# Blocks of two chunks in the attention layer of a four-layer graph kernel

## The chip, the cores and the metric

The kernel runs on one core of a Trainium2 chip, as one program and one launch. The metric is the device time of an execution in microseconds (us). The engines of a core run their own queues and meet at semaphores: TensorE (matmuls into PSUM), VectorE (elementwise work), ScalarE (copies and activations), GpSimd, and SyncE, which issues most transfers. In the profile they are PE, DVE, ACT, POOL and SP; PEld is TensorE's load of weights, the stationary operand.

## The reference, cut to what matters

Four layers update `x` (2708 rows of 256). Each adds a graph operation to `x` and normalises the rows. The change lies in layer 1, attention of four heads of 64 over the edges of `adj`:

```python
h = (x @ W).reshape(n, heads, head_dim)
src = jnp.einsum('nhd,d->nh', h, a[:head_dim, 0])
dst = jnp.einsum('nhd,d->nh', h, a[head_dim:, 0])
e = src[:, :, None] + dst.T[None, :, :]
e = jnp.where(e > 0, e, ALPHA * e)
e = jnp.where(adj[:, None, :] > 0, e, NEG_INF)
attn = jax.nn.softmax(e, axis=-1)
out = jnp.einsum('nhm,mhd->nhd', attn, h).reshape(n, heads * head_dim)
out = (out - mu) / jnp.sqrt(var + LN_EPS) * gamma + beta
```

For every row and head a sum of weighted rows of `h` is needed, and the total of the weights, its denominator.

## The kernel before

The 2708 rows are 22 tiles of 128 (the last has 20 rows). The program is traced with a framework that assigns buffers, sets semaphores and orders each engine's queue by a planner: an instruction earlier in the program goes first, but one whose operands are ready in the plan can be put ahead of it. A pool with `bufs=n` for a tag hands out n buffers in turn; a tile that takes a used buffer waits for its last reader.

**What layer 1 holds.** The exponential of the leaky logit splits into a factor of the row and a factor of the column, and a maximum of two such products. `rise` has a column value per neighbour and head (a chunk is one tile of 128 neighbours, on the partitions); `fall_b` has the row factors of a group of rows, the same on all partitions, loaded from the DRAM tensor `fall_d` by `load_fall` (L418 to L421); `mask` says where an edge is. One VectorE instruction (L835) makes the weights of a chunk of neighbours for all rows of a group and one head, the tile `p`: the larger of `fall_b` and `rise`, times `mask`. `hs[c]` holds, for each head, the rows of `h` of chunk c, scaled, with the scale itself as an added column.

**Groups and passes.** The rows are taken in groups of two spans, `for g in range(0, len(spans), 2)` (L786): spans of 512 and 512 rows, again 512 and 512, and last 384 and 276. A group makes two passes over the 22 chunks, one for each pair of heads q (L810), so there are six passes. In a pass each chunk does:

- two weight tiles `p` (heads 2q and 2q+1) on VectorE, from a pool of five buffers (L834);
- `heads` (L814): for both spans and both heads a matmul with 64 columns of `hs` as the weights and a span's columns of `p` as the moving operand, into accumulators `acc[s]`. The two heads fill two halves of the array side by side;
- `totals` (L822): the same with the last 32 columns of a head's `hs`, whose last column gives the denominator. The four of a chunk (two spans, two heads) fill four quarters side by side and go into one accumulator `den`.

Each such matmul is two instructions on TensorE[...]. The order of the parts turns at each chunk (L841): totals then heads for even chunks, heads then totals for odd ones, so that equal parts of neighbouring chunks meet.

After the first part of a chunk, `step(c)` (L796) does one piece of other work: in the first group what remains of layer 0, in later ones the end of the group before (`layer1_end`, L683, and `layer1_logits`, L748: transposes and small matmuls on TensorE, a few instructions on VectorE, many on ScalarE). For the first pair of heads it starts a piece where c leaves 1 when divided by 5, for the second where c is a multiple of 5.

**End of a pass.** ScalarE copies `acc` to `sum` (L848) and `den` to `den0` and `den1` (L852). The pool of accumulators has four banks, a pass uses three, and the next pass takes what is free.

**Row factors.** `falls` (L623) holds two tiles of four heads by 1024 columns, loaded on GpSimd's queue as soon as layer 0 has done their rows (L449). The third group's takes the first one's buffer, on SyncE's queue (L789 to L792).

After the last pass the memory of layer 1 goes to `raw_sums` (L354), whose loads `pa` start layer 2.

Of the kernel before, what the change touches and what calls it, by code (L numbers as in the profile page):

```python
# [9 lines left out]
F32 = mybir.dt.float32  # L10
# [5 lines left out]
ALU = mybir.AluOpType  # L16
# [3 lines left out]
P = 128  # L20
# [7 lines left out]
def kernel(  # L28
# [24 lines left out]
    nc = tc.nc  # L53
    N, F = x.shape
    NT = -(-N // P)
    FC = F // P
    HD = a1.shape[0] // 2
    H = F // HD
# [3 lines left out]
    W = GT * P  # L62
    CT = 32
# [6 lines left out]
    spans = [(sum(sizes[:i]), sum(sizes[: i + 1])) for i in range(len(sizes))]  # L70
# [21 lines left out]
    def width(lo, hi):  # L92
        return min(hi * P, N) - lo * P
# [9 lines left out]
                yield t, a, b  # L103
            lo -= sz(t)

    def bcast_rows(d, lo, n):

        return bass.AP(tensor=d.tensor, offset=d.offset + lo, ap=[[0, P], [d.shape[1], d.shape[0]], [1, n]])

    def pool(name, bufs=1, **kw):  # L110
        return tc.tile_pool(name=name, bufs=bufs, reuse_waits="tile", **kw)
# [32 lines left out]
    fall_d = dram.tile([H, N], F32, name="fall_d")  # L144
# [253 lines left out]
    mask = mask_pool.tile([P, NT, MP], FP8, name="mask")  # L398
# [5 lines left out]
    if True:  # L404
# [6 lines left out]
        rise = keep.tile([P, NT, H], F32, name="rise")  # L411
# [3 lines left out]
        ps_t = ps_t_stack.enter_context(pool("ps_t", 4, space=PSUM, side="right"))  # L415
        ps_acc = acc_stack.enter_context(pool("ps_acc", 4, space=PSUM))
        if True:
            def load_fall(dst, g, queue):  # L418
                at, w = spans[g][0] * P, width(*spans[g])
                off = at - spans[g - g % 2][0] * P  # L420
                queue.dma_start(dst[:, :, off : off + w], bcast_rows(fall_d, at, w))  # L421

            def layer1_projection(pool, t):
                n = sz(t)
                xt = transposed(ps_t, pool, xs[t], n, "xt")
                yield
                pm = ps_t.tile([P, 4, P], F32, tag="tr", name="pm").rearrange("p i q -> p (i q)")
                for f in range(FC):
                    nc.tensor.matmul(
                        pm[:n, : F + 2 * H], xt[:, f, :n], w1_a[:, f], start=(f == 0), stop=(f == FC - 1)  # L430
                    )
                nc.scalar.activation(rise[:n, t, :], pm[:n, F + H : F + 2 * H], AF.Exp, scale=1.0 - ALPHA)
                nc.scalar.activation(hs[t][:n, :, HD], pm[:n, F + H : F + 2 * H], AF.Exp, scale=ALPHA)
                fall = pool.tile([P, H], F32, tag="fall", name="fall", bufs=4)
                nc.scalar.activation(fall[:n], pm[:n, :H], AF.Exp, scale=ALPHA - 1.0)
                nc.vector.tensor_tensor(
                    hs[t][:n, :, :HD],
                    pm[:n, H : H + F].rearrange("p (h d) -> p h d", d=HD),
                    hs[t][:n, :, HD:].to_broadcast([n, H, HD]),
                    ALU.mult,  # L440
                )
                yield
                pf = ps_t.tile([P, 4, P], F32, tag="tr", name="pf")
                nc.tensor.transpose(pf[:H, 0, :n], fall[:n], ident[:n, :n])
                turned = pool.tile([H, P], F32, tag="turned", name="turned")
                nc.scalar.copy(turned[:, :n], pf[:H, 0, :n])
                nc.gpsimd.dma_start(fall_d[:, t * P : t * P + n], turned[:, :n])

                for g in [g for g, (lo, hi) in enumerate(spans[:4]) if hi == t + 1]:  # L449
                    load_fall(falls[g // 2], g, nc.gpsimd)  # L450

            w0_b = keep.tile([P, F], F32, name="w0_b")
            quarter = keep.tile([P, CT], F32, name="quarter")
# [2 lines left out]
            with pool("l0", 2) as l0:  # L456
# [48 lines left out]
                with pool("prep", side="right") as prep:  # L505
# [3 lines left out]
                    for c0, c1 in blocks:  # L509
                        whole = min(c1, N // P)  # L510
                        queue = nc.scalar if c1 <= 3 else nc.sync
# [33 lines left out]
                    for f in range(FC):  # L545
                        for s in range(2):
# [7 lines left out]
                            at = s * (H + F)  # L554
# [50 lines left out]
                    t = ahead + 1  # L605
# [14 lines left out]
                gamma_b = keepr.tile([P, F], F32, name="gamma_b")  # L620
                beta_b = keepr.tile([P, F], F32, name="beta_b")
                fallp = fall_stack.enter_context(pool("fallp", 2, side="right"))
                falls = [fallp.tile([P, H, 2 * W], F32, tag="fall_b", name="fall_b") for _ in range(2)]  # L623
                nc.sync.dma_start(gamma_b, bcast(gamma, F))
                nc.sync.dma_start(beta_b, bcast(beta, F))
                layer0_scale(ahead, last)
# [10 lines left out]
                t = NT - 1  # L637
# [23 lines left out]
            if True:  # L661
# [124 lines left out]
                for g in range(0, len(spans), 2):  # L786
                    segs = spans[g : g + 2]
                    at, w = segs[0][0] * P, width(segs[0][0], segs[-1][1])
                    if g >= 4:  # L789
                        falls.append(fallp.tile([P, H, 2 * W], F32, tag="fall_b", name="fall_b"))  # L790
                        for i in range(len(segs)):
                            load_fall(falls[-1], g + i, nc.sync)  # L792
                    cols = [(lo * P - at, width(lo, hi)) for lo, hi in segs]
                    sums, steps, halves = [], [itertools.chain(*rest)] if g == 0 else [], []

                    def step(c):  # L796
                        for s in list(steps):
                            if next(s, s) is s:
                                steps.remove(s)

                        if q == 0 and c % 5 == 1 and len(halves) < len(ended):
                            halves.append(layer1_end(l1, ended[len(halves)]))
                            next(halves[-1])
                            steps.append(itertools.islice(halves[-1], 2))

                        if q == 1 and c % 5 == 0 and c // 5 < len(halves):
                            steps.append(itertools.chain(halves[c // 5], [None], layer1_logits(ended[c // 5])))
                            next(steps[-1])

                    for q in range(H // 2):  # L810
                        den = ps_acc.tile([P, W], F32, tag="acc", name="den")
                        acc = [ps_acc.tile([P, W], F32, tag="acc", name="acc") for _ in segs]

                        def heads(c, ps, flags):  # L814
                            for s, (p0, ws) in enumerate(cols):
                                for i in (1, 0):
                                    nc.tensor.matmul(  # L817
                                        acc[s][i * HD : (i + 1) * HD, :ws], hs[c][:, 2 * q + i, :HD],
                                        ps[i][:, p0 : p0 + ws], **flags,
                                    )  # L820

                        def totals(c, ps, flags):  # L822
                            for s, (p0, ws) in enumerate(cols):
                                for i in (1, 0):
                                    j = (2 * (s ^ q) + i) * CT
                                    nc.tensor.matmul(  # L826
                                        den[j : j + CT, :ws], hs[c][:, 2 * q + i, HD + 1 - CT :],
                                        ps[i][:, p0 : p0 + ws], **flags,
                                    )

                        for c in range(NT):
                            ps = []
                            for i in range(2):
                                p = l1.tile([P, 2 * W], F32, tag="p", name="p", bufs=5)  # L834
                                nc.vector.scalar_tensor_tensor(  # L835
                                    p[:, :w], falls[g // 2][:, 2 * q + i, :w], rise[:, c, 2 * q + i : 2 * q + i + 1],
                                    mask[:, c, at : at + w], ALU.max, ALU.mult,
                                )
                                ps.append(p)

                            for part in (heads, totals)[:: -1 if c % 2 == 0 else 1]:  # L841
                                part(c, ps, dict(start=(c == 0), stop=(c == NT - 1)))
                                if part is (totals, heads)[c % 2]:
                                    step(c)
                        got = []
                        for s, (p0, ws) in enumerate(cols):
                            sb = keepr.tile([P, W], F32, tag=f"sum{q}{s}", name=f"sum{q}{s}")
                            nc.scalar.copy(sb[:, :ws], acc[s][:, :ws])  # L848
                            got.append(sb)
                        for s, (p0, ws) in enumerate(cols):  # L850
                            two = slice(2 * (s ^ q) * CT, 2 * ((s ^ q) + 1) * CT)
                            nc.scalar.copy(dens[s][two, :ws], den[two, :ws])  # L852
                        sums.append(got)
                    for a in steps:
                        for _ in a:
                            pass
                    ended = [(t, s, sums, dens, t - segs[0][0]) for s, (lo, hi) in enumerate(segs) for t in range(lo, hi)]
                    ended = [ended[i : i + 2] for i in range(0, len(ended), 2)]
# [842 lines left out]
```

## Time and profile before

| | |
|---|---|
| median of three runs | 1865.03 us (1864.9 to 1866.25) |
| profiled execution, its own time | 1865.35 us |
| its span (first to last instruction) | 1863.6 us |
| granted TensorE clock | 0.998 |
| layer 1, first totals to last | 247.06 to 590.5 us, 343.4 us |

The six passes, each from its first totals matmul to that of the next (busy us):

| pass | from to | length | PE | DVE | ACT |
|---|---|---|---|---|---|
| group 1, heads 0 and 1 | 247.06 to 308.31 | 61.25 | 61.25 | 56.87 | 1.98 |
| group 1, heads 2 and 3 | 308.31 to 368.31 | 60.00 | 60.00 | 54.75 | 2.41 |
| group 2, heads 0 and 1 | 368.31 to 431.36 | 63.05 | 63.05 | 60.58 | 26.15 |
| group 2, heads 2 and 3 | 431.36 to 497.46 | 66.10 | 66.10 | 54.01 | 9.31 |
| group 3, heads 0 and 1 | 497.46 to 542.33 | 44.87 | 44.87 | 42.86 | 22.57 |
| group 3, heads 2 and 3 | 542.33 to 590.50 | 48.17 | 47.94 | 37.99 | 11.53 |

In a row of the profile's tables of groups stand line, engine, operation, output and inputs, tile shape and count, then busy time in us, mean ns of one, and the idle time before it with what ended it. In the order of time a row begins with start and duration in us. A PE matmul that is called 128*64 uses 128 partitions and 64 columns of weights. Matmuls overlap, so their durations can't be added; starts can be compared.

### The profile page before, as it was taken

Reading aid. Unit: us, or ns where it says so; the run is one execution under the profiler, and the core shown is the slowest. Engines: PE = TensorE matmul, PEld = TensorE weight load, DVE = VectorE, ACT = ScalarE, POOL = GpSimd, SP = SyncE. Lnnn points to the kernel's source line nnn. Section 1 sums busy time; section 2 is a strip of 40 time slices with the busy share of each in tenths; the row PEclk is TensorE's granted clock in tenths of the full one; section 3 lists DMA queues with packets and bytes.
Section 4 is the critical chain, followed back from the end, with each engine's and each line's share of the span. In section 5 each row is a group of like instructions: output and inputs, shape, how many; then the busy total and the mean of one; then the engine's idle time right before and its main releaser. Section 6 shows DMA issues by size and latency. Waiting matters only on the chain. (4 is left out here: it accounts for less than half of the span.)

```text
span 1863.6 us, 23088 instructions
## 1 busy us (share of the span) xinstructions
PE 1832.7 (98%) x7526; PEld 1035.4 (56%) x7530; DVE 1280.9 (69%) x2263; ACT 699.3 (38%) x1442; POOL 266.4 (14%) x427
## 2 busy tenths in 40 slices
PE   9999999999999999999999999999999999999997
PEld 7788832233345887887444444444445556654555
DVE  5344489999897664754568888776887768844664
ACT  3544410033144203111546655555665556321011
POOL 1211220001012411000002000111200302111111
PEclk9999999999999999999999999999999999999999
DMA  8344410100002667754647666454554545634764
GB/s 298 133 148 151 168 30 1 30 1 12 12 7 71 144 144 186 182 130 114 182 131 207 176 174 171 123 159 114 165 151 121 135 106 141 167 106 116 203 163 121
DMA packets 435101, 237.32 MB, mean 127 GB/s; under 512 B 184363, under 2 KB 422348, under 8 KB 432540
## 3 DMA queue, kind: packets, MB, share of 16 engines
q1 hardware_dynamic: 422414, 208.66, 41.4%
q0 software_dynamic: 8208, 22.59, 3.9%
q10 hardware_dynamic: 4350, 4.50, 0.7%
q8 instruction: 62, 1.02, 0.2%
q14 instruction: 67, 0.55, 0.1%
HBM read 223.00 MB, written 12.66 MB: 126 GB/s over the span
## 5 line engine op out<-in xcount | busy, mean ns | idle before, releaser
L835 DVE SCALAR_TENSOR_TENSOR p<-fall_b,rise,mask 128x1024 f32<-128x1024 f32 (+1 forms) x264 | 293.9, 1156 | 32.5 <-PE den L826 16.7
L1328 ACT ACTIVATE p<-st,e_neg 128x1024 f32<-128x1024 f32 (+1 forms) x198 | 197.3, 1040 | 193.9 <-PE m L328 190.1
L328 PE MATMUL m<-s,xq 128*128 128x512 f32 (+3 forms) x660 | 230.1, 467 | 0.0
L817 PE MATMUL acc<-p,h 128*64 128x512 f32 (+2 forms) x1056 | 214.5, 548 | 0.2 <-ACT sum L848 0.2
L328 PE MATMUL m<-p,xq 128*128 128x512 f32 (+1 forms) x396 | 183.0, 544 | 0.1
L215 PE MATMUL acc<-turn,strip 128*128 128x257 f32 x792 | 181.8, 379 | 0.0
L1331 ACT ACTIVATE p<-p 128x1024 f32<-128x1024 f32 (+1 forms) x198 | 178.8, 942 | 0.2
L315 DVE TENSOR_TENSOR s<-p 128x512 f32<-128x512 f32 (+3 forms) x132 | 81.5, 618 | 136.6 <-PE m L328 112.7
L328 PE MATMUL m<-p,x 128*128 128x512 f32 (+1 forms) x396 | 167.7, 542 | 0.3 <-DVE supt L345 0.3
L328 PEld LDWEIGHTS m<-s,xq 128*128 128x128 f32 x660 | 124.5, 190 | 76.3 <-issue 59.2
L1332 DVE TENSOR_TENSOR p<-p,blk 128x1024 f32<-128x1024 f32 (+1 forms) x132 | 142.8, 1101 | 33.6 <-ACT p L1331 23.1
L215 PEld LDWEIGHTS acc<-turn,strip 128*128 128x128 f32 x792 | 147.2, 190 | 20.3
L817 PEld LDWEIGHTS acc<-p,h 128*64 128x64 f32 x1056 | 69.8, 136 | 138.2 <-issue 128.6
L328 PE MATMUL m<-s,x 128*128 128x512 f32 (+3 forms) x330 | 127.2, 467 | 0.0
L826 PE MATMUL den<-p,h 128*32 128x512 f32 (+2 forms) x1056 | 117.8, 548 | 0.0
L328 PEld LDWEIGHTS m<-p,xq 128*128 128x128 f32 x396 | 74.6, 190 | 76.9 <-issue 61.3
L328 PEld LDWEIGHTS m<-p,x 128*128 128x128 f32 x396 | 74.8, 190 | 75.5 <-issue 61.1
L474 ACT ACTIVATE below<-strip 128x384 bf16<-128x384 f32 x132 | 78.4, 594 | 68.4 <-DMA strip<-in_adj_t_dram 65.0
L316 DVE TENSOR_TENSOR p<-p 128x512 f32<-128x512 f32 (+3 forms) x132 | 82.3, 624 | 2.3
L328 PEld LDWEIGHTS m<-s,x 128*128 128x128 f32 x330 | 62.0, 190 | 39.2 <-issue 34.6
L318 DVE TENSOR_TENSOR s<-p,s 128x512 f32<-128x512 f32 (+3 forms) x132 | 81.2, 615 | 1.9
L286 POOL TENSOR_TENSOR blk<-blk,offdiag 128x128 f32<-128x128 f32 (+3 forms) x50 | 28.2, 566 | 376.0 <-DMA blk<-in_adj_t_dram 359.2
(288 smaller groups left out, 2591.9 us busy)
## 6 DMA issues: line engine op xcount, KB each, us to landing
strip<-in_adj_t_dram SPq DMA_DIRECT2D x19, 1408.0 KB, 6.0
blk<-in_adj_t_dram SPq DMA_DIRECT2D x88, 256.0 KB, 3.4
blk<-in_adj_t_dram SPq DMA_DIRECT2D x88, 192.0 KB, 4.1
pa<-in_adj_t_dram SPq DMA_DIRECT2D x110, 128.0 KB, 2.8
turn<-in_adj_t_dram SPq DMA_DIRECT2D x44, 256.0 KB, 3.1
blk<-in_adj_t_dram SPq DMA_DIRECT2D x88, 128.0 KB, 2.7
p<-in_adj_t_dram SPq DMA_DIRECT2D x88, 128.0 KB, 2.7
turn<-in_adj_t_dram SPq DMA_DIRECT2D x44, 192.0 KB, 3.1
```

The lines of the kernel that those rows point to most:

```text
L215: at = nc.tensor.matmul(acc, s[:, c, :n], rhs(c), start=(c == 0), stop=(c == NT - 1))
L315: nc.vector.tensor_tensor(s1, a21, a22, ALU.add)
L316: nc.vector.tensor_tensor(a21, a21, a11, ALU.subtract)
L318: nc.vector.tensor_tensor(s4, a12, s2, ALU.subtract)
L328: nc.tensor.matmul(dst[:, :w], lt, rt, start=start and not (one_bank and i), stop=stop and not (one_bank and i in (1, 2, 5)))
L474: nc.scalar.activation(below[:, : (hi - lo) * P], s[:, lo:hi].rearrange("p c n -> p (c n)"), AF.Relu, scale=-1.0, accum_out=negative[:, BE ...
L817: nc.tensor.matmul(acc[s][i * HD : (i + 1) * HD, :ws], hs[c][:, 2 * q + i, :HD], ps[i][:, p0 : p0 + ws], **flags,)
L826: nc.tensor.matmul(den[j : j + CT, :ws], hs[c][:, 2 * q + i, HD + 1 - CT :], ps[i][:, p0 : p0 + ws], **flags,)
L835: nc.vector.scalar_tensor_tensor(p[:, :w], falls[g // 2][:, 2 * q + i, :w], rise[:, c, 2 * q + i : 2 * q + i + 1], mask[:, c, at : at + w] ...
L1328: nc.scalar.activation(p[:, :, :w], st_k[:, :, :w], AF.Relu, scale=-1.0, bias=e_neg[:, at, k : k + 1])
L1331: nc.scalar.activation(p[:, :, :w], p[:, :, :w], AF.Exp, scale=-1.0)
L1332: nc.vector.tensor_tensor(p[:, :, :w], p[:, :, :w], blk[:, i, :, :w], ALU.mult)
```

## The change

Layer 1's chunks are taken in blocks of two. An even block does the totals of both chunks, then the heads of both; an odd block heads, then totals. `step` is called after the first part for the first chunk and after the second part for the second. The pool of `p` has nine buffers in place of five. A tile of `fall_b` holds only the two heads of one pass; the two of the first group are loaded in layer 0, and each later one at the end of the pass that used its buffer. In the last group the totals no longer follow the spans of 384 and 276 rows but stretches of 320 and 340, and the copies of `den` put the rows back to their spans; in the other groups the stretches are 512 and 512, as before.

```diff
-    def bcast_rows(d, lo, n):
+    def bcast_rows(d, row, rows, lo, n):
 
-        return bass.AP(tensor=d.tensor, offset=d.offset + lo, ap=[[0, P], [d.shape[1], d.shape[0]], [1, n]])
+        return bass.AP(tensor=d.tensor, offset=d.offset + row * d.shape[1] + lo, ap=[[0, P], [d.shape[1], rows], [1, n]])
...
-            def load_fall(dst, g, queue):
+            def load_fall(dst, g, q, queue):
...
-                queue.dma_start(dst[:, :, off : off + w], bcast_rows(fall_d, at, w))
+                queue.dma_start(dst[:, :, off : off + w], bcast_rows(fall_d, 2 * q, 2, at, w))
...
-                for g in [g for g, (lo, hi) in enumerate(spans[:4]) if hi == t + 1]:
-                    load_fall(falls[g // 2], g, nc.gpsimd)
+                for g in [g for g, (lo, hi) in enumerate(spans[:2]) if hi == t + 1]:
+                    for q, dst in enumerate(falls):
+                        load_fall(dst, g, q, nc.gpsimd)
...
-                falls = [fallp.tile([P, H, 2 * W], F32, tag="fall_b", name="fall_b") for _ in range(2)]
+                falls = [fallp.tile([P, 2, 2 * W], F32, tag="fall_b", name="fall_b") for _ in range(H // 2)]
...
-                    if g >= 4:
-                        falls.append(fallp.tile([P, H, 2 * W], F32, tag="fall_b", name="fall_b"))
-                        for i in range(len(segs)):
-                            load_fall(falls[-1], g + i, nc.sync)
                     cols = [(lo * P - at, width(lo, hi)) for lo, hi in segs]
+                    cut = min(cols[1][0], (w // 2 + P // 4) // (P // 2) * (P // 2))
+                    halves_at = [(0, cut), (cut, w - cut)]
...
                         def totals(c, ps, flags):
-                            for s, (p0, ws) in enumerate(cols):
+                            for s, (p0, ws) in enumerate(halves_at):
...
-                        for c in range(NT):
-                            ps = []
-                            for i in range(2):
-                                p = l1.tile([P, 2 * W], F32, tag="p", name="p", bufs=5)
-                                nc.vector.scalar_tensor_tensor(
-                                    p[:, :w], falls[g // 2][:, 2 * q + i, :w], rise[:, c, 2 * q + i : 2 * q + i + 1],
-                                    mask[:, c, at : at + w], ALU.max, ALU.mult,
-                                )
-                                ps.append(p)
-
-                            for part in (heads, totals)[:: -1 if c % 2 == 0 else 1]:
-                                part(c, ps, dict(start=(c == 0), stop=(c == NT - 1)))
-                                if part is (totals, heads)[c % 2]:
-                                    step(c)
+                        fall_b = falls.pop(0)
+                        for b, c0 in enumerate(range(0, NT, 2)):
+                            block = {}
+                            for c in range(c0, min(c0 + 2, NT)):
+                                block[c] = []
+                                for i in range(2):
+                                    p = l1.tile([P, 2 * W], F32, tag="p", name="p", bufs=9)
+                                    nc.vector.scalar_tensor_tensor(
+                                        p[:, :w], fall_b[:, i, :w], rise[:, c, 2 * q + i : 2 * q + i + 1],
+                                        mask[:, c, at : at + w], ALU.max, ALU.mult,
+                                    )
+                                    block[c].append(p)
+
+                            for i, part in enumerate((heads, totals)[:: -1 if b % 2 == 0 else 1]):
+                                for c, ps in block.items():
+                                    part(c, ps, dict(start=(c == 0), stop=(c == NT - 1)))
+                                if c0 + i < NT:
+                                    step(c0 + i)
+                        if g + 2 < len(spans):
+                            falls.append(fallp.tile([P, 2, 2 * W], F32, tag="fall_b", name="fall_b"))
+                            for i in range(len(spans[g + 2 : g + 4])):
+                                load_fall(falls[-1], g + 2 + i, q, nc.sync)
...
-                            nc.scalar.copy(dens[s][two, :ws], den[two, :ws])
+                            for i, (a, n) in enumerate(halves_at):
+                                lo, hi = max(p0, a), min(p0 + ws, a + n)
+                                if lo < hi:
+                                    part = slice(2 * (i ^ q) * CT, 2 * ((i ^ q) + 1) * CT)
+                                    nc.scalar.copy(dens[s][two, lo - p0 : hi - p0], den[part, lo - a : hi - a])
```

## The prediction

> **What bounds the kernel now.** I read the page first, then the table of the span by stretches, then the order of time on TensorE and on its weight loads inside layer 1, and last the waits. The page's busy line and its two largest groups of layer 1:
>
> ```profile
> PE 1832.7 (98%) x7526; PEld 1035.4 (56%) x7530; DVE 1280.9 (69%) x2263; ACT 699.3 (38%) x1442; POOL 266.4 (14%) x427
> ...
> L835 DVE SCALAR_TENSOR_TENSOR p<-fall_b,rise,mask 128x1024 f32<-128x1024 f32 (+1 forms) x264 | 293.9, 1156 | 32.5 <-PE den L826 16.7
> ...
> L817 PE MATMUL acc<-p,h 128*64 128x512 f32 (+2 forms) x1056 | 214.5, 548 | 0.2 <-ACT sum L848 0.2
> ```
>
> TensorE (PE) is busy all the time and waits for nobody; VectorE (DVE) waits 32.5 us, for TensorE to give weight tiles back. A busy TensorE still says nothing of gaps inside it, so I go to the order of time. TensorE in the pass of the second group, first pair of heads:
>
> ```profile
> 380.99 3.65 PE L817 MATMUL acc<-p,h 128*64 128x512 f32 x16
> 384.57 1.92 PE L826 MATMUL den<-p,h 128*32 128x512 f32 x16
> ...
> 387.23 3.65 PE L817 MATMUL acc<-p,h 128*64 128x512 f32 x16
> 390.82 1.93 PE L826 MATMUL den<-p,h 128*32 128x512 f32 x16
> 392.67 3.65 PE L817 MATMUL acc<-p,h 128*64 128x512 f32 x16
> ```
>
> Every program matmul is two instructions, so x16 is two chunks. The reader is to see strict alternation: heads of two chunks, totals of two chunks. Now the weight loads of one such pair of runs:
>
> ```profile
> 380.99 0.20 PEld L817 LDWEIGHTS acc<-p,h 128*64 128x64 f32 x4 [0.84 <-issue]
> 381.47 0.14 PEld L817 LDWEIGHTS acc<-p,h 128*64 128x64 f32 x2 [0.29 <-issue]
> 381.90 0.14 PEld L817 LDWEIGHTS acc<-p,h 128*64 128x64 f32 x2 [0.29 <-issue]
> ...
> 384.57 0.16 PEld L826 LDWEIGHTS den<-p,h 128*32 128x32 f32 x8 [0.81 <-issue]
> 385.03 0.13 PEld L826 LDWEIGHTS den<-p,h 128*32 128x32 f32 x4 [0.30 <-issue]
> ...
> 386.43 0.20 PEld L694 LDWEIGHTS tr<-ident,sum 128*128 128x128 f32 x2 [0.84 <-issue]
> ```
>
> Loads inside a run start 0.43 us apart: one slot of 512 columns, two heads matmuls or four totals matmuls side by side. A run of heads over two chunks is 8 slots, 3.44 us, but lasts 380.99 to 384.57, 3.58; a run of totals is 4 slots, 1.72, but lasts 1.86, to the first transpose of other work at 386.43. Each change of kind thus costs 0.14 us beyond its slots. In the last group the slot of 384 columns is 0.32 us; runs there start thus:
>
> ```profile
> 537.90 1.49 PE L826 MATMUL den<-p,h 128*32 128x384 f32 x16
> 539.32 2.44 PE L817 MATMUL acc<-p,h 128*64 128x384 f32 x16
> ```
>
> Totals: 1.42 us for 4 slots of 0.32 and one change. The 276-column matmuls of the totals set nothing; they run beside the 384-column ones.
>
> Check by sum: a wide pass is 22 x (4 + 2) x 0.43 + 22 x 0.14 = 59.8 us, and the second pass, which has no other work in it, is 60.0 long. So layer 1 is slots plus changes, with no stall.
>
> **What the Trainium skill says.** "TensorEngine Tiling (Array Packing)", section Tiling Modes, Key Properties: "Changing tiling mode (not just tile) drains the TensorE". It gives no price; this trace agrees and prices it at 0.14 us. "TensorE: Matmul & The Clock Gate", Part 3, says that column tiles run concurrently while matmuls start and end in program order; the trace agrees: four 32-column totals share one slot. "Trainium Kernel Development and Optimization", Performance Expectations, warns that matmul busy time measures little since matmuls are pipelined; hence the weight loads above. No page that I use bears on the weight-tile buffers.
>
> **The change, part by part.**
>
> *Blocks of two chunks.* Even blocks do totals of two chunks, then heads of two; odd blocks the reverse. Equal kinds of neighbouring blocks join, so a run is four chunks long. Eleven blocks have eleven inner changes, and one more falls between passes (a pass now ends with heads and starts with totals): 12 against 22. Six passes x 10 x 0.14 us = 8.4 us off TensorE.
>
> *Stretches of 320 and 340.* A totals slot in the last group falls from 384 to 340 columns. At 0.43/512 = 0.84 ns a column, 44 columns x 2 slots = 0.074 us a chunk, x 44 chunks of two passes = 3.25 us off.
>
> *Steps inside a run.* The planned extra work (transposes, small matmuls of L694, L756, L773) is called after the first and the second part of a block. Before, every such place was a change of kind anyway. Now the second is inside a run of four chunks, and the work breaks it: one more change. In the passes that carry the end of the former group the calls that use TensorE come at chunks 1, 6, 11, 16 (first pair) and 4, 5, 9, 10, 14, 15, 19, 20 (second pair); half are odd chunks, 12 in all over two groups, and some 2 for the last rows of layer 0 in the first pass: 14 x 0.14 = 2.0 us back.
>
> *End of a pass.* Before, the last run was totals of one chunk, so the ScalarE copies of the sums went beside it. Now heads end last; the four copies (0.59 us each, 2.4 with a wake of 0.25 makes 2.6) must free accumulators while the next pass does two chunks of totals, 1.72 + 0.28 us. If the heads wait for two sums alone, that is hidden; if for all four copies, 0.6 us late. Nothing to 3.1 us over five ends; I take 0.2 each, 1.0. The third denominator copy in the last group sits on ScalarE, busy 34.1 us of the 93.0 in those passes: nothing.
>
> *Nine weight buffers.* A block holds four tiles until its second part, so five would not carry it; nine hold the block and 2.5 chunks ahead. VectorE's need is what could take over. By pass of the last two groups:
>
> ```profile
> 368.31:431.36 63.05, 63.05 (x380) 18.80 (x376) 60.58 (x86) 26.15 (x128) 8.44 (x7) 1.00 0.04 13
> 431.36:497.46 66.10, 66.10 (x404) 21.81 (x400) 54.01 (x48) 9.31 (x25) 6.34 (x9) 1.00 0.06 17
> 497.46:542.33 44.87, 44.87 (x382) 20.36 (x378) 42.86 (x80) 22.57 (x119) 5.16 (x5) 1.00 0.00 1
> 542.33:590.50 48.17, 47.94 (x404) 23.21 (x394) 37.99 (x55) 11.53 (x34) 10.05 (x20) 1.00 0.07 22
> ```
>
> Length, then busy PE, weight loads, DVE, ACT and POOL. The third pass needs 60.6 us of VectorE and will have 63.05 - 1.4 + 0.3 = 61.95 of TensorE: still TensorE, by little. The fifth needs 42.9 and will have 44.87 - 1.4 - 1.63 + 0.3 = 42.1: VectorE falls 0.8 us behind, from a lead of 2.5 chunks, where a chunk of 660 columns is 1.72 us of VectorE. The lead mostly covers it: 0.5 us, between nothing and 3.0 if an epilogue instruction blocks weights behind it. Gain from the deeper buffers: TensorE's few waits for p are 4.5 us in sum at most 0.3 long, mostly inside a slot; I count none, at best 1.5.
>
> *Row factors.* Six half-sized tiles in place of three: the same bytes. Two heads are loaded on SyncE's queue at the end of each of the first four passes, after VectorE's last read of the slot, and needed one whole pass (about 60 us) later; such a load lands in 5.5 to 6.6 us, and that queue stands idle in layer 1. On GpSimd's queue in layer 0 it is still four loads, of half the size. Nothing. It would cost up to 6 us a pass only were the load placed behind something on SyncE that waits for the end of layer 1; none is there before 590.77.
>
> Sum: 8.4 + 3.25 - 2.0 - 1.0 - 0.5 = 8.15 us. The stages after layer 1 start when its last matmul frees buffers (their first loads go out at 590.77, 0.3 us after it) and TensorE is the bound there too, so all shifts with it. Against the profiled execution, 1865.35 (1863.6 of span and 1.75 around it): 1857.2. The median of the runs is 0.3 lower, 1865.03: 1856.9.
>
> **Rivals.**
>
> *VectorE and the accumulators take part of it back.* Both upper bounds come in: 3.1 for 1.0 and 3.0 for 0.5. Gain 3.55 us, 1861.5. For: the narrow margins of the third and fifth pass. Against: the second pass of each group leaves VectorE idle 10 us or more, which refills its lead.
>
> *The drain is not saved.* If the 0.14 us comes back inside longer runs (weights queued too late), only 3.25 - 1.5 is left: 1863.3. Against: inside the present runs the step over a chunk's end shows no gap, 0.43 throughout.
>
> *The order is not the written one (slower).* The planner that orders the queues is free to take heads of a chunk that are ready before totals of the next that are not. If each chunk's totals and heads then alternate, TensorE changes 44 times a pass: 22 x 6 x 0.14 = 18.5 us more, less 3.25: 1880. It decides from about 24 changes a pass on, where 12 extra changes eat the remaining 1.75 us. For: it does reorder; VectorE works on L727 at 379.99, a whole pass ahead of its place in the program. Against: that hoisting shows weights planned well ahead of TensorE, and TensorE itself runs in written order in every pass before.
>
> **How the numbers follow.** Forecast 0.66, first rival 0.12, second 0.10, third 0.10, better than all bounds 0.02. The forecast's own ends are 1853.9 (no cost at the ends of passes or from VectorE, 1.5 gained by buffers) and about 1860. The range 1853.5 to 1863.5 takes in the first two rivals and leaves out the third: some 0.86. A measurement of this kernel tells 0.2%, 3.7 us, from no change: below 1861.3 lie the forecast, half of the first rival and the rest, 0.74; within are the other half and the second rival, 0.16; slower is the third, 0.10.
>
> **What would show it.** Right: TensorE runs of x32 for heads and totals in the middle of a pass, 0.43 apart inside; the second pass 58.5 long; totals of the last group 0.57 a chunk; layer 1 ending near 582. Wrong: waits of TensorE for p or for the sums' copies above 3 us in sum, VectorE without idle time in the third or fifth pass, runs of x8, or a later start of the first matmul on pa than 3.3 us after layer 1.

## The result, and the profile after

| | before | after |
|---|---|---|
| median of 18 runs each, side by side | 1866.07 us (1863.38 to 1869.16) | 1859.25 us (1856.86 to 1865.58) |
| ratio, with its 95% interval | | 0.9968 [0.9961, 0.9975] |
| profiled execution, its own time | 1865.35 us | 1862.97 us |
| its span | 1863.6 us | 1861.2 us |

The changed kernel is faster by 0.32%, some 6.0 us, where 8.15 us were forecast. The means of the 18 runs differ by 6.05 us, the medians by 6.82. The forecast of 1856.9 us lies 2.35 us below the median.

The page of after, in the lines that answer to those of before (busy lines, then groups: busy time, mean ns of one, idle time before and its cause):

```profile
PE 1825.8 (98%) x7530; PEld 1040.5 (56%) x7530; DVE 1275.9 (69%) x2263; ACT 699.3 (38%) x1444; POOL 266.6 (14%) x427
...
L837 DVE SCALAR_TENSOR_TENSOR p<-fall_b,rise,mask 128x1024 f32<-128x1024 f32 (+1 forms) x264 | 288.0, 1153 | 25.7 <-PE den L825 15.1
...
L816 PE MATMUL acc<-p,h 128*64 128x512 f32 (+2 forms) x1056 | 210.1, 547 | 0.0
```

The picture is the old one: TensorE has no idle time of its own before the heads, and VectorE still waits for weight tiles to come back, now 25.7 us instead of 32.5. So VectorE has not become the bound. This page can't show more, since the saved drains were counted as busy.

The table of after by stretches, one row for each pass (length, busy PE, weight loads, DVE, ACT, POOL, granted clock, DMA share, GB/s):

```profile
250.45:312.42 61.97, 61.97 (x363) 17.59 (x362) 59.31 (x59) 2.63 (x9) 4.98 (x6) 1.00 0.09 26
312.42:370.80 58.38, 58.38 (x355) 17.21 (x353) 53.14 (x46) 2.33 (x4) 0.00 (x0) 1.00 0.06 19
370.80:432.69 61.89, 61.89 (x379) 19.55 (x377) 59.68 (x83) 25.76 (x126) 8.20 (x6) 1.00 0.04 12
432.69:497.78 65.09, 65.09 (x403) 22.48 (x401) 54.03 (x54) 9.78 (x26) 7.22 (x10) 1.00 0.09 28
497.78:540.01 42.23, 42.23 (x377) 21.11 (x376) 38.64 (x70) 20.00 (x110) 4.71 (x4) 1.00 0.00 1
540.01:588.62 48.61, 47.06 (x402) 24.09 (x401) 35.94 (x59) 14.53 (x45) 11.02 (x20) 0.96 0.07 20
```

Against the passes of before, and against what the prediction's terms give for each (0.14 us for ten changes, the cut, the broken runs, 0.2 for an end, 0.5 for VectorE in the fifth):

| pass | before | after | change | forecast |
|---|---|---|---|---|
| 1 | 61.25 | 61.97 | +0.72 | -0.92 |
| 2 | 60.00 | 58.38 | -1.62 | -1.20 |
| 3 | 63.05 | 61.89 | -1.16 | -0.92 |
| 4 | 66.10 | 65.09 | -1.01 | -0.64 |
| 5 | 44.87 | 42.23 | -2.64 | -2.05 |
| 6 | 48.17 | 48.61 | +0.44 | -2.47 |
| sum | 343.44 | 338.17 | -5.27 | -8.20 |

Four passes gain a little more than the forecast, and two gain nothing. Those two are what has to be explained. In the last row of the table by stretches the reader is to see 48.61 beside a busy time of 47.06, and a clock of 0.96: TensorE waited there and then ran slower.

Outside layer 1 nothing is gained. From the end of layer 1 to the first matmul on `pa` it takes 3.0 us, before 3.25, and what follows is as long as it was. But layer 1 begins at 250.45 us in this profile, at 247.06 in that of before, although of layer 0 the change touches only the loads of row factors; the last section comes back to it. That is why the two profiled executions lie only 2.4 us apart; this one is also 3.7 us slower than the median of its kernel.

The order of time on TensorE in the second pass of after (start, duration, matmuls):

```profile
353.06 3.64 PE L825 MATMUL den<-p,h 128*32 128x512 f32 x32
356.63 7.09 PE L816 MATMUL acc<-p,h 128*64 128x512 f32 x32
363.64 3.64 PE L825 MATMUL den<-p,h 128*32 128x512 f32 x32
```

These are the runs of four chunks: 3.57 us from start to start for 8 slots of 0.43 and a change, 7.01 for 16 slots and a change. In the first pass of after the same view reads otherwise:

```profile
251.84 1.94 PE L816 MATMUL acc<-p,h 128*64 128x512 f32 x8
253.71 1.07 PE L825 MATMUL den<-p,h 128*32 128x512 f32 x8
254.70 5.37 PE L816 MATMUL acc<-p,h 128*64 128x512 f32 x24
260.00 2.78 PE L825 MATMUL den<-p,h 128*32 128x512 f32 x24
262.71 1.08 PE L816 MATMUL acc<-p,h 128*64 128x512 f32 x4
```

This isn't the written order. Heads of chunk 0 (x8) stand before totals of chunk 1, so the runs hold one, one, three, three and half a chunk. The whole pass has 18 changes of kind where the written order has 12, and small matmuls of layer 0 break its runs in five places instead of two. The planner put ahead what was ready, which is the prediction's third rival, in one pass only.

The last pass of after, around its one wait (order of time over all engines, so lines overlap; in brackets, idle time before and what ended it):

```profile
561.64 0.66 PE L757 MATMUL tr<-ident,x 128*128 128x128 f32 x4
561.87 1.23 POOL L681 TENSOR_TENSOR o_rs<-o_var,neg_half 128x2 f32<-128x2 f32 x1 [7.55 <-DVE o_var L680]
...
562.22 1.35 PE L825 MATMUL den<-p,h 128*32 128x320 f32 x16
...
563.14 0.48 ACT L744 ACTIVATE o_mean<-o_mean,o_rs 128x1 f32<-128x1 f32 x2 [3.89 <-POOL o_rs L681]
...
563.52 1.07 ACT L745 ACTIVATE x<-turn,o_mean,o_rs 128x256 f32<-128x256 f32 x2
564.51 0.56 ACT L759 COPY turn<-tr 128x512 f32<-128x512 f32 x1
...
565.12 1.05 PE L774 MATMUL pm<-uw,turn 128*128 128x3 f32 x8 [1.54 <-ACT turn L759]
...
566.10 2.49 PE L825 MATMUL den<-p,h 128*32 128x320 f32 x16
...
568.52 5.15 PE L816 MATMUL acc<-p,h 128*64 128x384 f32 x32
```

The small matmuls `pm` need ScalarE's copy of the transposes (L759). The transposes end at 562.30, but the copy starts only at 564.51: it stands in ScalarE's queue behind L744 and L745, which serve another pair of tiles and wait for GpSimd's L681, which itself waited for VectorE's L680. All that TensorE has to do between is the totals of two chunks, 1.28 us from start to `pm`'s place. It then waits 1.54 us. And the same totals of two chunks take 2.42 us after the wait, the heads of four chunks 5.08 us from start to start instead of 4.59: another 1.6 us, at the lower clock. The pass of before in this place, over all engines:

```profile
563.74 0.66 PE L756 MATMUL tr<-ident,x 128*128 128x128 f32 x4
...
564.32 2.44 PE L817 MATMUL acc<-p,h 128*64 128x384 f32 x16
564.43 0.59 ACT L758 COPY turn<-tr 128x512 f32<-128x512 f32 x1 [1.99 <-PE tr L756]
...
565.92 0.48 ACT L743 ACTIVATE o_mean<-o_mean,o_rs 128x1 f32<-128x1 f32 x2 [0.91 <-POOL o_rs L680]
...
566.69 1.05 PE L773 MATMUL pm<-uw,turn 128*128 128x3 f32 x8
```

Two things differ. There the heads of two chunks, 2.37 us, lay between; the blocks put totals in this place, and the cut made these narrower. And there the copy (L758 in that kernel) started as soon as the transposes had ended, ahead of L743, the L744 of after; in after it starts 2.2 us after their end. It takes both to make a wait of this size. With the longer cover some 0.45 us of it would be left (an estimate, 1.54 less the 1.09 us of cover), and the next piece of work in the same pass has the short cover, a prompt copy and no wait:

```profile
574.88 0.66 PE L757 MATMUL tr<-ident,x 128*128 128x128 f32 x4
...
575.47 1.35 PE L825 MATMUL den<-p,h 128*32 128x320 f32 x16
575.78 0.56 ACT L759 COPY turn<-tr 128x512 f32<-128x512 f32 x1
...
576.75 1.05 PE L774 MATMUL pm<-uw,turn 128*128 128x3 f32 x8
```

### The profile page after: what moved, and what is told of

Same layout as the page of the kernel before. It is cut to its first block, busy times and chain, and to the rows that moved or that the text cites. A ratio compares the mean times of both kernels' runs of the same rounds, so it can differ in the third digit from the quotient of the medians.

```text
span 1861.2 us, 23102 instructions
## 1 busy us (share of the span) xinstructions
PE 1825.8 (98%) x7530; PEld 1040.5 (56%) x7530; DVE 1275.9 (69%) x2263; ACT 699.3 (38%) x1444; POOL 266.6 (14%) x427
## 4 chain that ended last, share of the span: by engine, by line
PE 87%; DMA 5%; DVE 3%; SPq 2%; ACT 1%; issue 1%; POOL 0%; POOLq 0%; DVEq 0%; ACTq 0%
PE m L328 42%; PE acc L816 11%; PE acc L215 7%; PE bank L1198 7%; PE den L825 6%; PE gate L1073 4%; PE bank L1174 3%; DMA strip<-in_adj_t_dram 2%; PE bank L1241 2%; SPq L275 1%; DMA p<-in_adj_t_dram 1%; PE pm L429 1%; ACT below L475 1%; PE pq L994 1%; PE m L1439 1%
## 5 line engine op out<-in xcount | busy, mean ns | idle before, releaser
L837 DVE SCALAR_TENSOR_TENSOR p<-fall_b,rise,mask 128x1024 f32<-128x1024 f32 (+1 forms) x264 | 288.0, 1153 | 25.7 <-PE den L825 15.1
L816 PE MATMUL acc<-p,h 128*64 128x512 f32 (+2 forms) x1056 | 210.1, 547 | 0.0
L825 PE MATMUL den<-p,h 128*32 128x512 f32 (+2 forms) x1056 | 113.5, 551 | 0.0
```

Source lines behind the costliest of these rows:

```text
L816: nc.tensor.matmul(acc[s][i * HD : (i + 1) * HD, :ws], hs[c][:, 2 * q + i, :HD], ps[i][:, p0 : p0 + ws], **flags,)
L825: nc.tensor.matmul(den[j : j + CT, :ws], hs[c][:, 2 * q + i, HD + 1 - CT :], ps[i][:, p0 : p0 + ws], **flags,)
L837: nc.vector.scalar_tensor_tensor(p[:, :w], fall_b[:, i, :w], rise[:, c, 2 * q + i : 2 * q + i + 1], mask[:, c, at : at + w], ALU.max, ALU. ...
```

## The experiments

The first four experiments ran side by side with one set of runs of the kernel before (32 runs, median 1865.18 us), the last four with another (11 runs, 1867.11 us). Each ratio is to its own set, and medians can be compared within a set.

### What a change of kind costs, the cut alone, and single chunks with nine buffers

The kernel before, with totals first in every chunk, so that TensorE changes kind 44 times a pass:

```diff
-                            for part in (heads, totals)[:: -1 if c % 2 == 0 else 1]:
+                            for part in (totals, heads):
                                 part(c, ps, dict(start=(c == 0), stop=(c == NT - 1)))
-                                if part is (totals, heads)[c % 2]:
+                                if part is totals:
                                     step(c)
```

> The kernel before, but every chunk does totals, then heads, so TensorE changes kind 44 times a pass in place of 22; the matmuls themselves are the same. If each change costs a drain of 0.14 us: 22 x 6 x 0.14 = 18.5 us slower, ratio to before about 1.010. If the drain comes back inside longer runs, or only part of it belongs to the change: below 5 us, ratio under 1.003.

Measured: 1.0098 [1.0082, 1.0113], a median of 1883.2 us. TensorE in its second pass, order of time:

```profile
313.00 1.94 PE L817 MATMUL acc<-p,h 128*64 128x512 f32 x8
314.87 1.07 PE L826 MATMUL den<-p,h 128*32 128x512 f32 x8
315.86 1.94 PE L817 MATMUL acc<-p,h 128*64 128x512 f32 x8
```

A chunk takes 2.86 us, six slots of 0.43 and two changes of 0.14. The ratio is 18.3 us for 132 added changes, 0.139 us each; in the profile layer 1 is 18.5 us longer. The price that four starts had given holds over the whole layer. It agrees with the sentence of the Trainium skill that it was put under ("TensorEngine Tiling (Array Packing)", Tiling Modes): a changed mode drains TensorE, here for 0.14 us.

The kernel before, with the stretches of the last group alone:

```diff
+                    cut = min(cols[1][0], (w // 2 + P // 4) // (P // 2) * (P // 2))
+                    halves_at = [(0, cut), (cut, w - cut)]
...
-                            for s, (p0, ws) in enumerate(cols):
+                            for s, (p0, ws) in enumerate(halves_at):
...
-                            nc.scalar.copy(dens[s][two, :ws], den[two, :ws])
+                            for i, (a, n) in enumerate(halves_at):
+                                lo, hi = max(p0, a), min(p0 + ws, a + n)
+                                if lo < hi:
+                                    part = slice(2 * (i ^ q) * CT, 2 * ((i ^ q) + 1) * CT)
+                                    nc.scalar.copy(dens[s][two, lo - p0 : hi - p0], den[part, lo - a : hi - a])
```

> The kernel before with one part of the change alone: totals of the last group in stretches of 320 and 340. If a slot of four totals lasts as long as its widest: 44 chunks x 2 slots x 44 columns x 0.84 ns = 3.25 us faster, ratio about 0.9983, all of it in the last two passes. If something else sets the slot: no change.

Measured: 0.9984 [0.9977, 0.9991], 1862.06 us: 3.0 us, where 3.25 were worked out; in the profile layer 1 is 3.1 us shorter. The cut pays by itself.

The changed kernel with the loop over single chunks of before; cut, row factors of one pass and nine buffers stay:

```diff
-                        for b, c0 in enumerate(range(0, NT, 2)):
...
+                        for c in range(NT):
+                            ps = []
+                            for i in range(2):
+                                p = l1.tile([P, 2 * W], F32, tag="p", name="p", bufs=9)
...
+                            for part in (heads, totals)[:: -1 if c % 2 == 0 else 1]:
+                                part(c, ps, dict(start=(c == 0), stop=(c == NT - 1)))
+                                if part is (totals, heads)[c % 2]:
+                                    step(c)
```

> The changed kernel without its blocks: one chunk at a time in the order of the kernel before, with nine weight buffers, the half row factors and the 320 and 340 stretches kept. If buffers and row factors are worth nothing in themselves: as the stretches alone, 3.25 us faster, ratio about 0.9983. If the deeper buffers also take away TensorE's short waits for p: up to 1.5 us more, 0.9975. If blocks are worth nothing: as the changed kernel, 0.9968.

Measured: 0.9988 [0.9980, 0.9997], 1862.22 us, the cut alone to within 0.2 us. Four more buffers and other row factors do nothing where chunks run singly. What the blocks themselves bring is thus the way from 0.9988 to the 0.9968 of the changed kernel, some 3.7 us, where the prediction had 8.15 - 3.25 = 4.9. These two ratios are not from the same set of runs, so this figure is rough: with the 0.9957 that the changed kernel shows further down it would be 5.8.

### The written order kept on TensorE

The changed kernel, in which each part of a chunk may be issued only after the part that stands before it in the program:

```diff
-                                    part(c, ps, dict(start=(c == 0), stop=(c == NT - 1)))
+                                    with tc.issue_after(done.ins) if done else ExitStack():
+                                        done = part(c, ps, dict(start=(c == 0), stop=(c == NT - 1)))
```

(`heads` and `totals` return their last matmul for it.)

> The changed kernel with each part of a block tied behind the part before it on TensorE, so that the planner can't take heads ahead of totals in the first pass. If the broken order of the first pass costs only its extra changes (22 in place of some 14): 1.1 to 1.4 us faster than the changed kernel, ratio to before about 0.9961, first pass about 60.6 us long in place of 62.0. If the planner broke the order because the weights really come late: TensorE waits for p there instead, and the pass is as long as before or longer, ratio 0.9968 or above.

TensorE in its first pass, order of time:

```profile
252.09 1.02 PE L826 MATMUL den<-p,h 128*32 128x512 f32 x5
253.28 1.06 PE L826 MATMUL den<-p,h 128*32 128x512 f32 x8 [0.17 <-DVE p L840]
254.27 7.09 PE L816 MATMUL acc<-p,h 128*64 128x512 f32 x32
261.29 3.64 PE L826 MATMUL den<-p,h 128*32 128x512 f32 x32
```

Now TensorE waits 0.17 us for the weights of chunk 1 and then has its long runs. The pass is 60.77 us long (251.65 to 312.42) instead of 61.97, so the broken order cost 1.20 us in the profile. The time says less: 0.9964 [0.9950, 0.9977], 1857.83 us, and the interval takes in the changed kernel's 0.9968. Its profile has the last pass's wait too, 1.55 us, but no lower clock after it: that pass is 47.0 us long. So the next two runs are the changed kernel once more, and a kernel without that wait.

### The wait of the last pass

The changed kernel again, unchanged:

> The changed kernel once more, unaltered, to see which parts of its profiled execution come back. If the wait of 1.54 us of the small matmul (pm) for ScalarE in the last pass is built in: it is there again, near 13 us before the middle of that pass's end, and the pass is 47 to 49 us long. If layer 0's late end (250.45 in place of 247.06) belongs to single executions: another value between 247 and 252. Ratio about 0.9968 in both cases.

Measured: 0.9957 [0.9943, 0.9971], 1858.12 us. Its last pass, TensorE in order of time:

```profile
560.31 0.66 PE L757 MATMUL tr<-ident,x 128*128 128x128 f32 x4
560.89 1.35 PE L825 MATMUL den<-p,h 128*32 128x320 f32 x16
563.79 1.05 PE L774 MATMUL pm<-uw,turn 128*128 128x3 f32 x8 [1.55 <-ACT turn L759]
564.78 1.35 PE L825 MATMUL den<-p,h 128*32 128x320 f32 x16
```

The wait is the same to 0.01 us, so it is built in. The totals after it take 1.28 us, so the lower clock is not. This pass is 46.99 us long, the first one 61.97 as in the other profile.

Then the same kernel with the small matmuls one call of `step` further from their transposes:

```diff
                         nc.gpsimd.dma_start(d[:, :, t * P - at : t * P - at + n], xt[:, i, :, :n])
                     yield
+                    yield
```

> The changed kernel with one more step between the transposes of layer1_logits and the small matmuls that read their copy, so that a whole block lies between them. If the lost time of the last pass is that wait and the lower clock after it: 1.5 to 3.1 us faster than the changed kernel, ratio to before 0.9952 to 0.9960, last pass about 45.5 us long. If the time is lost to VectorE's lead there: the wait moves to the weight tiles p and the ratio stays 0.9968.

Measured: 0.9944 [0.9931, 0.9958], 1855.59 us. Its last pass, the same place:

```profile
558.27 0.65 PE L757 MATMUL tr<-ident,x 128*128 128x128 f32 x4
558.86 2.49 PE L826 MATMUL den<-p,h 128*32 128x320 f32 x32
561.28 1.05 PE L775 MATMUL pm<-uw,turn 128*128 128x3 f32 x8
562.27 4.66 PE L817 MATMUL acc<-p,h 128*64 128x384 f32 x32
```

Totals of four chunks now lie between, nobody waits, and the pass is 45.51 us long: 2.66 less than before, where the prediction had 2.47. The fourth pass, which holds the same pieces, is 0.15 us longer (65.24), which is an added change of kind. The copy still stands behind the other pair's work, starting 1.5 us after the transposes' end, so it is the longer cover that hides it. Against the repetition the median is 2.5 us lower, within the 1.5 to 3.1 us expected; the ratio lies below the expected 0.9952 because the repetition itself came out at 0.9957. The profiles' layer 1 is 1.3 us shorter (335.23 against 336.55).

Both edits together:

> Both edits: parts tied in their written order, and the small matmuls one step later. If both losses are separate: 1.2 plus 1.5 to 3.1 us faster than the changed kernel, ratio to before 0.9945 to 0.9954, layer 1 about 333.5 us long. If they overlap: no better than the better of the two alone.

Measured: 0.9943 [0.9930, 0.9957], 1854.19 us, the lowest of all. Its passes are 60.77, 58.38, 61.89, 65.24, 42.23 and 45.51 us, in sum 334.0: 9.4 us less than before. The gains of the two edits add up in the profile. The last step, 1.4 us of median against the kernel with the late small matmuls alone, is what the first pass predicts (1.20), but the two intervals overlap almost wholly; the trace shows it, the times alone don't.

### Seven weight buffers

```diff
-                                    p = l1.tile([P, 2 * W], F32, tag="p", name="p", bufs=9)
+                                    p = l1.tile([P, 2 * W], F32, tag="p", name="p", bufs=7)
```

> The changed kernel with seven weight buffers in place of nine, so that VectorE can be at most 1.5 chunks ahead of a block in place of 2.5. If VectorE's lead is what keeps the third and the fifth pass from waiting: waits for p there, 2 to 4 us slower than the changed kernel, ratio to before 0.998 to 0.999, mostly in the last group. If nine are more than is needed: 0.9968.

Measured: 0.9967 [0.9956, 0.9978], 1861.05 us, 2.9 us above the repetition with nine. The waits of weight loads for weights in layer 1 (total us, times, longest), first with seven buffers:

```profile
PEld den L825 <- DVE p L837: 13.9, 27, 0.8
```

and with nine, in the repetition:

```profile
PEld den L825 <- DVE p L837: 3.9, 10, 0.8
```

Seven tiles hold the block's four and a lead of a chunk and a half, and VectorE's pauses for other work then reach TensorE. Most of these waits lie under running matmuls. Against the profile of the repetition the third, fifth and last pass are 0.20, 0.64 and 2.28 us longer (62.09, 42.87 and 49.27 us); some 1.7 us of the last figure is again a lower clock (0.97 in that pass). The times leave the price open: the ratio is the one that was expected if nine are more than is needed, not the 0.998 to 0.999 expected if VectorE's lead matters, and its interval overlaps that of the repetition.

## Why the prediction was right, and where its sum was off

**The bound.** It was TensorE, as said: every gain came out of its runs, and VectorE did not take over.

**"Six passes x 10 x 0.14 us = 8.4 us off TensorE."** The price held (0.139 us over 132 changes) and the count held in five passes: with their waits gone, passes 2 to 6 lose 1.62, 1.16, 0.86, 2.64 and 2.66 us in the kernel with both edits. In the first pass the count failed. Its 1.4 us were not saved, and the pass came out 0.72 us longer than before, because the planner took heads that were ready before totals whose weights were not. The prediction had this as its third rival and argued that "TensorE itself runs in written order in every pass before". That was true and proved nothing: with single chunks, the written order never asks TensorE for a later chunk's weights before an earlier chunk's heads. Blocks do, and at the start of layer 1 VectorE has no lead. With the order kept the pass is 1.20 us shorter, and still 0.44 longer than the forecast for it; waits for the first weights are left there.

**"Steps inside a run", 2.0 us.** Ten of the twelve broken runs that were counted in passes 3 to 6 are there; the other two calls fell on changes of kind. What was not priced is what lies between two steps. The sum has no term for the wait of `pm` on ScalarE: the prediction counted a change of kind for each misplaced step, and took for granted that the small matmuls would find their operand ready, as they did before. In the last pass one of them doesn't: a cover of heads (2.37 us) became one of narrowed totals (1.28 us), and the copy, which had started at once, now stands behind work that waits for GpSimd and starts 2.2 us after the transposes' end. That costs 1.5 us in both profiles of the kernel, and in the first one 1.6 more from the clock. The pass lost 2.91 us to its forecast, the largest single miss of that profile, and 1.29 in the repetition. That a longer cover hides the late copy is shown; why the planner placed the copy later was not tried.

**Ends of passes, 1.0 us, and VectorE, 0.5 us.** Neither was paid. No profile of the changed kernel shows TensorE waiting for the sums at a pass's end, and VectorE in the fifth pass has 38.64 us of work for 42.23, where 42.9 was taken: the table counts work in the pass in which it is done, and that can be ahead of the pass that needs it. These terms are most of the 1.62 us by which passes 2 to 5 beat their forecast, and that surplus paid for a third of the two misses (1.64 and 2.91 us), in the repetition for more than half (1.64 and 1.29). So the time came out close partly because terms were wrong in opposite directions, which is luck.

**The clock,** for which the sum has no term. The granted clock is on record for each execution: 0.9962 in the mean over the 18 of the changed kernel, 0.9975 and 0.9971 over the two sets of the kernel before, 0.9974 and 0.9972 over the five each with late small matmuls. A thousandth of 1860 us is 1.9 us, so by estimate some 2 us of the forecast gain went there; the lower clock after the wait of the last pass is a part of it.

**The cut, 3.25 us,** measured 3.0 alone. **Nine buffers:** no gain by themselves, as said; with seven TensorE's weight loads wait longer, but the times don't settle what that costs. **Row factors:** nothing, as said.

**The rivals.** VectorE and the accumulators taking part of it back: no. The drain not saved: no, runs of x32 have their slots of 0.43 us and one drain. The order not the written one: in one pass of six, far below the 24 changes in every pass from which the kernel would have been slower.

**The signs.** Runs of x32 came, and a second pass of 58.38 us where 58.5 was named; of the signs of being wrong, runs of x8 came, in the first pass. Layer 1 ends at 588.62 us and not near 582: it began 3.4 us later and gained 2.9 us less than forecast.

## What to carry to other kernels

An order that is written to save changes must be checked in the trace at its very start, where the producer has no lead, and the planner fills the hole with whatever is ready; pin it if a short wait is cheaper than the changes. When parts of a loop are regrouped, list for each small dependent matmul what now lies between it and the producer of its operand, and what stands ahead of that producer in its own queue: here a cover 1.1 us shorter and a copy 2.2 us later made a wait of 1.5 us, and the same short cover with a prompt copy made none. And a sum that comes out near the measured time still needs its terms looked at one by one, pass by pass.

## What the runs showed of the hardware

A TensorE wait of one to two microseconds can cost as much again after it, through the granted clock, and does not always. The table of after by stretches around the wait in the last pass (length, busy PE to POOL, granted clock, DMA share, GB/s):

```profile
565.00:566.00 1.00, 0.88 (x8) 0.88 (x8) 1.00 (x2) 0.77 (x4) 0.64 (x2) 1.00 0.00 0
566.00:567.00 1.00, 1.00 (x10) 0.51 (x13) 1.00 (x3) 0.16 (x1) 0.75 (x2) 0.57 0.41 127
567.00:568.00 1.00, 1.00 (x12) 0.26 (x4) 0.00 (x0) 0.80 (x3) 0.00 (x0) 0.50 0.44 135
568.00:569.00 1.00, 1.00 (x8) 0.30 (x4) 0.00 (x0) 0.00 (x0) 0.00 (x0) 0.50 0.00 0
569.00:570.00 1.00, 1.00 (x8) 0.43 (x6) 0.00 (x0) 0.00 (x0) 0.00 (x0) 0.73 0.00 0
570.00:571.00 1.00, 1.00 (x10) 0.51 (x8) 0.62 (x1) 0.00 (x0) 0.00 (x0) 1.00 0.00 0
```

The wait ends at 565.12, and from about 566.1 on the clock is halved. The missing shares of the four middle rows add up to 1.70 us (0.43, 0.50, 0.50, 0.27), which at half speed is a stretch of 3.4 us, and 1.70 is about the 1.63 us by which the matmuls there were late. After the wait of 1.40 us with seven buffers the rows read 0.71, 0.50, 0.50 and 0.58. After the one of 1.55 us in the repetition every row reads 1.00, and so it does after the 1.55 us in the kernel with the order pinned.

Layer 0, whose code is the same in all these kernels but for the loads of row factors, shows it too. A wait of 0.74 us near 50 us in the profile of before left the clock at 1.00. In that of after, TensorE reads

```profile
50.68 0.37 PE L444 MATMUL pf<-ident,fall 128*4 128x128 f32 x1 [2.32 <-DVE h L436]
```

and the clock by microseconds from 50 on is 0.86, 0.50, 0.50, 0.50 and 0.93: again 1.71 us missing. The waits of 2.24 us in the repetition and of 2.37 us with the order pinned cost as much; the one of 2.40 us with seven buffers cost nothing. In these four profiles layer 1 begins between 249.03 and 251.65 us. In the other six that wait is 0.74 to 1.73 us, the clock stays at 1.00, and layer 1 begins between 246.79 and 247.65. The four are all of the blocks with the small matmuls in their first place, yet the two kernels with late small matmuls have the same layer 0. With one profile of each it isn't shown whether the late start belongs to the kernel or to the execution, and why that wait differs was not tried.

The Trainium skill ("TensorE: Matmul & The Clock Gate", Part 1) says that the clock is halved after at least one idle window of about 3.4 us and comes back after a busy one, and that the windows run freely. The half and the 3.4 us of its return agree with these rows. The 3.4 us of idleness don't: waits of 1.40 to 2.37 us were enough. Even with the eight matmuls of three columns that follow the wait in the last pass, TensorE had little to do for 2.5 us only (563.57 to 566.10). That the same wait of 1.55 us can leave the clock alone would fit windows that run freely, but no run here tests that.
